# Issuing input loads from the sync engine's queue instead of the scalar engine's

## The chip, the cores and the metric

The kernel runs on one core of a Trainium2 chip. A core has five engines that run their own instruction streams in order and meet only at semaphores: TensorE (PE; its weight loads are shown apart as PEld), VectorE (DVE), ScalarE (ACT), GpSimd (POOL) and SyncE (SP). SP computes nothing here: it issues DMAs. ACT computes and can issue DMAs as well. An instruction that issues a DMA stands in its engine's stream like any other: if it has to wait, everything behind it in that stream waits. The metric is the device time of one execution in microseconds (us).

## The reference

The input `x` has 32 images of 32 channels, 128 x 128, in float32. There are two layers, each of the form x + f(groupnorm(x)), with groups of two channels (16 groups):

```python
x = x + _L0_conv_ref(_gn(x))
x = x + _L1_conv_ref(_gn(x), L1_conv_weights1, L1_conv_weights2)

# layer 0: per 128x128 matrix A, five Newton-Schulz steps towards its square root
Y = A / normA ; Z = I
for _ in range(5):
    T = 0.5 * (3.0 * I - Z @ Y)
    Y = Y @ T
    Z = T @ Z
return Y * sqrt(normA)

# layer 1: 2D FFT, keep 32 x 32 low modes at the top and bottom rows,
# mix the channels with a weight per mode, inverse FFT, real part
top = einsum('bixy,ioxy->boxy', x_dht[:, :, :32, :32], weights1)
bot = einsum('bixy,ioxy->boxy', x_dht[:, :, -32:, :32], weights2)
```

## The kernel before

**Sets.** Layer 0 works on sets of four channels of one image: 32 x 8 = 256 sets, in order. `fetch(b, g)` (line 367) loads a set twice from HBM: as it is (tile `b`, from `in_x`) and transposed (tile `xt`, from `in_xt`), 256 KB each. `staged` (line 375) normalises both in place or into tile `x`: ACT works on `b` and, for images 1 to 18, on half of `x`; POOL does the rest of `x`. `newton` (line 446) is a generator that takes the set through the products on PE, whose results DVE, ACT and POOL take out of PSUM; its last step adds the result to `xt`, and `settle` (line 483) stores `xt` to the scratch tensor `mid` (SP), folds it for layer 1 (POOL) and takes layer 1's statistics (DVE).

**Far and near.** Sets of images 1 to 18 ("far", by `is_far`, line 358) use `far_quartic` (line 421), the others `near_quartic` (line 407). Where the near one transposes on PE, the far one transposes 32 x 32 blocks on DVE (tile `turn`) and moves the blocks between partitions with four DMAs of 64 KB, issued by SP (tile `w <- turn`). A far set does this twice: 144 sets x 8 = 1152 DMAs. After them the set's generator rests four rounds before PE uses `w`.

**Statistics of layer 0.** `prep` (line 223) takes the statistics of one image (the first two) or of a pair of images. It reads the image from HBM in loads of 256 KB, 8 per image (`load`, line 234, tiles `xs`, in four buffers; for the first image four more loads go to `turn` buffers). Three loads are started at the outset and then one more after each load has been read by two `bn_stats` on DVE (`a_st <- xs`). The generator is stepped once a round in the first half of the kernel, every other round later.

**The order of the work** is the program's own: everything is issued through a wrapper (line 89, therefore the line that the profile shows for nearly all instructions) that keeps each engine's instructions in the order in which Python makes them. The main loop (line 1077) runs rounds. In each round it gives one step to each of eight lanes (one lane holds one set), and between the lanes one step to the staging of the next set, to `prep`, and to the queues of layer 1. A lane that takes a new set calls `stage` (line 1016), which begins the normalising of the next set and calls `fetch` for the one after it; so a set is fetched two sets before it starts. A far set starts every 23/8 rounds, a near one every 5.

**Layer 1** runs beside it: `forward` and `spectrum` per image, products with the weights per group of images (20, 7, 3 and 2), then `inverse` per image, which reads `mid` back (`yt`), adds the inverse transform (DVE and POOL) and stores `out`. Its DMAs (`mid`, `yt`, `out`, `ob`, `od`, the weights) are issued by SP; only in the tail ACT issues some.

**Which queue issues what.** Before the change ACT issues `b`, `xt` and `xs` (and `turn` for the first image); SP issues everything else.

Of the kernel before, what the change touches and what calls it, by code (L numbers as in the profile page):

```python
# [94 lines left out]
def conv_preact_kernel(  # L95
# [9 lines left out]
    nc = InOrder(tc)  # L105
# [74 lines left out]
    def bank():  # L180
        return ps8.tile([P, 4, P], F32, tag="ps", name="ps")

    def warm(n):
        ps = bank()
        for _ in range(n):
            nc.tensor.matmul(ps, ident, tab[:, 0:512], start=True, stop=True)

    def root(v, n, s):

        s0 = small.tile([P, n], F32, tag="root_0", name="root_0")  # L190
        nc.scalar.activation(s0, v, AF.Sqrt)
        yield
        q = small.tile([P, n], F32, tag="root_1", name="root_1")
        nc.vector.reciprocal(q, s0)
        nc.vector.tensor_mul(q, q, v)
        nc.vector.tensor_tensor(q, q, s0, ALU.add)
        nc.vector.tensor_scalar_mul(s, q, 0.5)

    def moments(st, ms, tag):

        n = st.shape[1]
        f = st.rearrange("p g (e t) -> p g e t", t=3)
        nc.vector.tensor_reduce(ms, f[:, :, :, 1], AX.X, ALU.add)
        yield from pause
        pm = bank()[:, 0, 0:n]
        nc.tensor.matmul(pm, avg_mean, ms, start=True, stop=True)
        nm = small.tile([P, n], F32, tag=f"{tag}_nm", name=f"{tag}_nm", bufs=2)
        nc.vector.tensor_scalar_mul(nm, pm, 2.0)
        d = small.tile([P, n, 2], F32, tag=f"{tag}_d", name=f"{tag}_d")
        nc.vector.tensor_tensor(  # L210
            d, f[:, :, :, 1], nm[:, :, None].to_broadcast([P, n, 2]), ALU.add
        )
        nc.vector.tensor_mul(d, d, d)
        nc.vector.scalar_tensor_tensor(d, d, 128.0, f[:, :, :, 2], ALU.mult, ALU.add)
        return nm, d
# [4 lines left out]
    def kept(issued):  # L220
        return issued

    def prep(bs, made):

        n = len(bs)
        nc_, ng = n * C, n * G
        first_b = bs[0]
        st = small.tile([P, ng, 6], F32, tag="a_st", name=f"a_st{first_b}", bufs=2)
        tiles = []
        parts = [(b, i) for b in bs for i in range(C // 4)]  # L230

        ahead = 3 if first_b else 8

        def load(k):
            b, i = parts[k]
            if first_b or i < 4:
                t = stp.tile([P, 2, 2 * P], F32, tag="xs", name=f"xs{b}_{i}")
            else:
                t = four("turn", True).rearrange("p (j c) x -> p j (c x)", j=2)
            src = xs_in[b, :, 2 * i : 2 * i + 2].rearrange("p g h c -> p g (h c)")  # L240
            kept(nc.scalar.dma_start(out=t, in_=src))
            tiles.append(t)

        for k in range(ahead):
            load(k)
        yield
        for k in range(len(parts)):
            for j in range(2):
                nc.vector.bn_stats(st[:, 2 * k + j, :], tiles[k][:, j, :])
            yield  # L250
            if k + ahead < len(parts):
                load(k + ahead)
        ms = small.tile([P, ng], F32, tag="a_ms", name=f"a_ms{first_b}")
        nm, d = yield from moments(st, ms, "a")
        yield from pause
        pq = bank()[:, 0, 0:nc_]
        nc.tensor.matmul(pq, avg_mean, d.rearrange("p g c -> p (g c)"), start=True, stop=True)
        if not first_b:
            warm(5)

        v = small.tile([P, nc_ + ng], F32, tag="a_v", name=f"a_v{first_b}")
        nc.vector.tensor_scalar_mul(v[:, 0:nc_], pq, -512 / (P * P))
        yield
        vg = small.tile([P, ng], F32, tag="a_vg", name=f"a_vg{first_b}")
        nc.vector.tensor_reduce(
            vg, v[:, 0:nc_].rearrange("p (g c) -> p g c", c=2), AX.X, ALU.add
        )
        nc.vector.tensor_scalar(v[:, nc_:], vg, 0.5, EPS, ALU.mult, ALU.add)
        yield
        s = small.tile([P, nc_ + ng], F32, tag="a_r_s", name=f"a_r_s{first_b}", bufs=2)  # L270
        yield from root(v, nc_ + ng, s)
        iv = small.tile([P, nc_ + ng], F32, tag="a_inv", name=f"a_inv{first_b}")
        nc.vector.reciprocal(iv, s)
        yield

        sc = small.tile([P, nc_], F32, tag="a_sc", name=f"a_sc{first_b}", bufs=2)
        nc.vector.tensor_scalar_mul(sc, iv[:, 0:nc_], MS / P)
        off = small.tile([P, ng, 2], F32, tag="a_off", name=f"a_off{first_b}", bufs=2)
        nc.vector.tensor_tensor(
            off,  # L280
            sc.rearrange("p (g c) -> p g c", c=2),
            nm[:, :, None].to_broadcast([P, ng, 2]),
            ALU.mult,
        )
        off = off.rearrange("p g c -> p (g c)")
        sn = small.tile([P, nc_], F32, tag="a_t_s", name=f"a_t_s{first_b}", bufs=3)
        for k, b in enumerate(bs):
            g, c = slice(k * G, k * G + G), slice(k * C, k * C + C)
            made[b] = (nm[:, g], sc[:, c], off[:, c], sn[:, c])
        yield  # L290
        nn = small.tile([P, ng, 2], F32, tag="a_d", name=f"a_n{first_b}")
        nc.vector.tensor_tensor(
            nn,
            s[:, 0:nc_].rearrange("p (g c) -> p g c", c=2),
            iv[:, nc_:, None].to_broadcast([P, ng, 2]),
            ALU.mult,
        )
        nn = nn.rearrange("p g c -> p (g c)")
        for far in sorted({is_far(b) for b in bs}):
            of = [k for k, b in enumerate(bs) if is_far(b) == far]  # L300
            c = slice(of[0] * C, of[-1] * C + C)
            f = EYE_Q * QS if far else EYE * QF
            nc.vector.tensor_scalar_mul(nn[:, c], nn[:, c], P * (1.5 / f) ** 2)
        yield
        yield from root(nn, nc_, sn)
        yield
# [6 lines left out]
    def four(tag, more):  # L313
        n, m = rooms[tag]
        shape = [P, 4, 2, P] if tag == "my" else [P, 4, P]
        if more:
            turns[tag] += 1
            if turns[tag] % (n + m) >= n:
                return early.tile(shape, F32, tag=tag + "_early", name=tag, bufs=m)
        return sets.tile(shape, F32, tag=tag, name=tag, bufs=n)  # L320
# [37 lines left out]
    def is_far(b):  # L358
        return 0 < b < FIRST

    def has_more(b, g):

        return b * (C // 4) + g < MORE
# [2 lines left out]

    def fetch(b, g):
        xt, t = four("xt", has_more(b, g)), four("b", has_more(b, g))
        kept(nc.scalar.dma_start(out=t, in_=x[b, :, 4 * g : 4 * g + 4, :]))
        kept(nc.scalar.dma_start(out=xt, in_=xt_in[b, :, 4 * g : 4 * g + 4, :]))  # L370
        raw[b, g] = xt, t

    norms = []
# [642 lines left out]
    def stage():  # L1016

        b, g = stages.pop(0)
        if g == 0:
            while b not in made:  # L1020
                step(preps)
        while coming and (b, g) >= coming[0][0]:
            preps.append(prep(coming.pop(0)[1], made))
        norms.append(staged(b, g, *made[b]))
        if fetches:
            fetch(*fetches.pop(0))
# [45 lines left out]
    step(preps)  # L1072
    coming = [((0, 0), [1])] + [((b - 2, 4 if b < FIRST else 2), [b, b + 1]) for b in range(2, B, 2)]
    fetch(*fetches.pop(0))
    stage()
    fetch(*fetches.pop(0))
    while todo or any(lanes) or posts or specs or prods or backs:
        tail = not todo and not any(lanes)
        if early and len(settled) >= MORE:
            change()  # L1080
        for i in range(LANES):
# [5 lines left out]
            if lanes[i] is None and todo and room and rounds >= due:  # L1087
# [3 lines left out]
                b, g = todo.pop(0)  # L1091
                xt = ready[0][0]
# [5 lines left out]
            if lanes[i] is not None:  # L1098
                b, g, xt, steps = lanes[i]
# [86 lines left out]
```

## Time and profile before

Three runs took 3022.42 us in the median (3022.03 to 3023.22). The profiled execution took 3016.65 us.

| what | value |
|---|---|
| profiled execution, its span | 3016.65 us, 3014.7 us |
| PE, PEld busy | 2897.6 us, 2689.0 us |
| DVE, POOL, ACT busy | 2321.8 us, 1995.8 us, 1652.1 us |
| queue of SP: packets, MB, share of the 16 DMA engines | 328512, 347.77, 38.7% |
| queue of ACT: the same | 113616, 208.45, 22.2% |
| `w<-turn` issues on SP | 1152 of 64 KB |
| `b<-in_x`, `xt<-in_xt` issues on ACT | 256 and 256 of 256 KB |
| `xs<-in_xs` issues on ACT | 252 of 256 KB |

How to read it: an engine's busy time does not count the issuing of DMAs or the waiting for semaphores. In the lists of waits a line names the engine and the tile that it was about to work on, then what ended its idle time, the total in us, how often, and the longest. `SPq` and `ACTq` are the issuing sequencers of SP and ACT. In the lines in order of time the columns are start (us from the span's start), duration (us), engine, operation, tiles, count, and in square brackets the idle time before and what ended it. All instructions are shown at line 89, the wrapper; so tiles tell them apart.

### The profile page before, as it was taken

To read this page: it belongs to the slowest core of one execution; us is meant where nothing else is said; L and a number is where in the kernel's file an instruction comes from. 1 tells how busy PE (TensorE), PEld (TensorE's weight loads), DVE (VectorE), ACT (ScalarE), POOL (GpSimd) and SP (SyncE) were. 2 spreads that over 40 slices of the span, in tenths; PEclk is the share of its full clock that TensorE was granted. 3 is DMA by queue.
4 is the path that set the end of the run, shared out by engine and by line. 5 is a ranking of instruction groups with operands and counts; after the bars stand their busy time and mean duration, and the time that the engine had idled before them with its cause. 6 is when DMAs were issued, how large, how long until landed. Compare 5 with 4: busy or idle time off the path is not lost.

```text
span 3014.7 us, 73315 instructions
## 1 busy us (share of the span) xinstructions
PE 2897.6 (96%) x27112; PEld 2689.0 (89%) x27112; DVE 2321.8 (77%) x4262; ACT 1652.1 (55%) x4187; POOL 1995.8 (66%) x2308
## 2 busy tenths in 40 slices
PE   7999999999999999999999999999989999999995
PEld 7899999999999999999999889888878899888884
DVE  7778898989888888889876645777886767776564
ACT  4566666566565656566554445455544544665452
POOL 4676777777777767777765434787777763678352
PEclk9999999999999999999999999999999999999997
DMA  5465655556565656565633566777877737676576
GB/s 176 135 176 145 171 163 153 167 152 180 134 192 135 192 131 195 142 183 140 190 102 99 158 209 208 257 247 254 271 235 245 252 121 225 203 242 216 175 230 242
DMA packets 442482, 560.91 MB, mean 186 GB/s; under 512 B 99344, under 2 KB 260112, under 8 KB 442128
## 3 DMA queue, kind: packets, MB, share of 16 engines
q1 hardware_dynamic: 328512, 347.77, 38.7%
q10 hardware_dynamic: 113616, 208.45, 22.2%
q8 instruction: 218, 3.57, 0.5%
q14 instruction: 136, 1.11, 0.1%
HBM read 326.93 MB, written 153.62 MB: 159 GB/s over the span
## 4 chain that ended last, share of the span: by engine, by line
PE 71%; POOL 8%; DVE 7%; DMA 7%; issue 5%; SPq 1%; ACT 1%; ACTq 0%; POOLq 0%; DVEq 0%
PE ps L89 71%; POOL yt L89 3%; POOL r L89 2%; POOL x L89 1%; POOL fold L89 1%; DMA yt<-mid 1%; SPq L89 1%; DVE turn L89 1%; DVE root L89 1%; DMA w<-turn 1%; DMA out<-yt 1%; DVE v L89 1%; DVE yt L89 1%; DVE a_d L89 1%; DMA xs<-in_xs 1%
## 5 line engine op out<-in xcount | busy, mean ns | idle before, releaser
L89 PE MATMUL ps<-my,q 128*128 128x128 f32 (+1 forms) x4096 | 747.0, 330 | 16.6 <-DVE q L89 9.9
L89 PEld LDWEIGHTS ps<-my,q 128*128 128x128 f32 x4096 | 623.0, 192 | 67.7 <-issue 7.4
L89 PE MATMUL ps<-w,v 128*128 128x128 f32 x4096 | 555.4, 279 | 19.6 <-DVE w L89 15.3
L89 ACT ACTIVATE b<-b,a_off,a_sc 128x128 f32<-128x128 f32 x1024 | 469.7, 491 | 166.2 <-issue 57.0
L89 ACT ACTIVATE my<-ps 128x512 f32<-128x512 f32 x512 | 306.2, 599 | 428.3 <-PE ps L89 408.9
L89 POOL TENSOR_TENSOR fold<-xt 128x256 f32<-128x256 f32 x512 | 363.4, 731 | 261.5 <-DVE xt L89 248.9
L89 PEld LDWEIGHTS ps<-w,v 128*128 128x128 f32 x4096 | 502.9, 193 | 32.5 <-DVE w L89 13.9
L89 POOL TENSOR_TENSOR yt<-yt,d 128x512 f32<-128x512 f32 x244 | 306.5, 1279 | 223.2 <-ACT d L89 195.5
L89 ACT ACTIVATE t<-ps 128x256 f32<-128x256 f32 x512 | 192.0, 381 | 311.7 <-PE ps L89 298.4
L89 DVE STREAM_TRANSPOSE turn<-v 128x512 f32<-128x512 f32 x288 | 326.1, 1132 | 9.9
L89 POOL TENSOR_SCALAR x<-xt,a_nm,a_sc 128x128 f32<-128x128 f32 x736 | 321.4, 450 | 15.6 <-DVE a_sc L89 15.4
L89 POOL TENSOR_TENSOR mb<-eye_q,mb 128x512 f32<-128x512 f32 x144 | 184.0, 1278 | 197.8 <-ACT y L89 139.2
L89 ACT ACTIVATE y<-ps,a_t_s 128x128 f32<-128x128 f32 x1024 | 290.4, 374 | 0.0
L89 POOL TENSOR_TENSOR v<-eye_v,x 128x512 f32<-128x512 f32 x144 | 184.0, 1278 | 143.8 <-ACT x L89 136.7
L89 PE MATMUL ps<-q,t 128*128 128x128 f32 x2048 | 273.9, 277 | 4.3 <-ACT t L89 3.7
L89 PE MATMUL ps<-x,b 128*128 128x128 f32 x2048 | 277.7, 279 | 0.0
L89 PE MATMUL ps<-x,q 128*128 128x128 f32 x2048 | 274.7, 277 | 3.0 <-DVE w L89 2.0
L89 DVE SCALAR_TENSOR_TENSOR v<-ps,v 128x512 f32<-128x512 f32 x288 | 195.1, 678 | 104.5 <-PE ps L89 101.8
L89 PE MATMUL ps<-y,t 128*128 128x128 f32 x2048 | 274.5, 277 | 0.1
L89 PE MATMUL ps<-my,mb 128*128 128x128 f32 x2048 | 272.2, 276 | 0.0
L89 PEld LDWEIGHTS ps<-my,mb 128*128 128x128 f32 x2048 | 257.9, 192 | 9.6 <-issue 1.6
L89 PEld LDWEIGHTS ps<-x,q 128*128 128x128 f32 x2048 | 249.4, 192 | 14.1 <-issue 8.4
(131 smaller groups left out, 5074.9 us busy)
## 6 DMA issues: line engine op xcount, KB each, us to landing
w<-turn SPq DMA_DIRECT2D x1152, 64.0 KB
b<-in_x ACTq DMA_DIRECT2D x256, 256.0 KB
xt<-in_xt ACTq DMA_DIRECT2D x256, 256.0 KB
mid<-xt SPq DMA_DIRECT2D x256, 256.0 KB
yt<-mid SPq DMA_DIRECT2D x128, 512.0 KB
xs<-in_xs ACTq DMA_DIRECT2D x252, 256.0 KB
out<-yt SPq DMA_DIRECT2D x115, 512.0 KB
plain<-in_wk SPq DMA_DIRECT2D x34, 512.0 KB
```

The lines of the kernel that those rows point to most:

```text
L89: return self.tc.keep_in_program_order(issue(*args, **kw))
```

## The change

Three calls that issue loads name the sync engine where they named the scalar engine. They stand at the same places of the source.

```diff
@@ prep, load(k)
             src = xs_in[b, :, 2 * i : 2 * i + 2].rearrange("p g h c -> p g (h c)")
-            kept(nc.scalar.dma_start(out=t, in_=src))
+            kept(nc.sync.dma_start(out=t, in_=src))
             tiles.append(t)
@@ fetch(b, g)
         xt, t = four("xt", has_more(b, g)), four("b", has_more(b, g))
-        kept(nc.scalar.dma_start(out=t, in_=x[b, :, 4 * g : 4 * g + 4, :]))
-        kept(nc.scalar.dma_start(out=xt, in_=xt_in[b, :, 4 * g : 4 * g + 4, :]))
+        kept(nc.sync.dma_start(out=t, in_=x[b, :, 4 * g : 4 * g + 4, :]))
+        kept(nc.sync.dma_start(out=xt, in_=xt_in[b, :, 4 * g : 4 * g + 4, :]))
         raw[b, g] = xt, t
```

## The prediction

> **What bounds the kernel now.** I read the busy totals first, then the stages, then who waits for whom, then two places in order of time.
>
> The page's first part and its chain:
>
> ```profile
> span 3014.7 us, 73315 instructions
> PE 2897.6 (96%) x27112; PEld 2689.0 (89%) x27112; DVE 2321.8 (77%) x4262; ACT 1652.1 (55%) x4187; POOL 1995.8 (66%) x2308
> PE 71%; POOL 8%; DVE 7%; DMA 7%; issue 5%; SPq 1%; ACT 1%; ACTq 0%; POOLq 0%; DVEq 0%
> ```
>
> TensorE is busy 96%; the scalar engine and its queue hold 1% and 0% of the chain, so freeing them cannot bring much. Busy time by stage (PE, PEld, DVE, ACT, POOL, then clock, DMA share, GB/s):
>
> ```profile
> 450.00:610.00 160.00, 159.27 (x1333) 151.22 (x1332) 139.02 (x245) 97.42 (x250) 116.23 (x129) 1.00 0.59 162
> 2080.00:2350.00 270.00, 256.51 (x2270) 231.27 (x2268) 210.54 (x386) 139.29 (x366) 205.37 (x234) 0.98 0.78 258
> ```
>
> There are two regimes. From 130 to 1510 us (images 1 to 18, one pair of images every 160 us) PE idles 0.7 us of 160, DVE is 87% busy, ACT 61%. After 1510 us PE idles some 5%. Over the whole span, gaps of more than 0.3 us in which neither PE nor its weight loads run sum to 89 us: 9 us between 130 and 1510, 53 between 1510 and 2790, 21 after, 6 before 130. A gain can only come out of these; a loss can come anywhere.
>
> Waits between 290 and 1410 us, DVE's and SP's own:
>
> ```profile
> DVE a_st L89 <- DMA xs<-in_xs: 10.0, 12, 1.7
> SPq L89 <- DVE turn L89: 354.0, 105, 7.1
> ```
>
> DVE already meets the statistics' loads (xs) late 12 times. SP spends 354 us waiting for a block's `turn` tile: a load put behind such a wait inherits it. One such place, in order of time:
>
> ```profile
> 349.73 0.33 ACTq L89 DMA_DIRECT2D xs<-in_xs  x1
> 349.97 6.28 SPq L89 DMA_DIRECT2D w<-turn  x8
> ...
> 353.46 0.75 DVE L89 BATCH_NORM_STATS2 a_st<-xs 128x6 f32<-128x256 f32 x2 [0.88 <-DMA xs<-in_xs]
> ```
>
> And one where the present order hurts:
>
> ```profile
> 2300.58 1.02 ACTq L89 DMA_DIRECT2D xs<-in_xs  x2
> 2301.65 0.60 ACT L89 ACTIVATE my<-ps 128x512 f32<-128x512 f32 x1 [7.78 <-issue]
> ...
> 2302.30 1.99 PEld L89 LDWEIGHTS ps<-my,q 128*128 128x128 f32 x9 [4.51 <-ACT my L89]
> ```
>
> ACT stood 7.8 us before a copy out of PSUM because two loads ahead of it in its stream could not issue, and PE then idled 4.1 us.
>
> **What the Trainium skill says.** "DMA: Bandwidth & Descriptors", section "Anatomy of one DMA": the engines that move data do not wait on semaphores; the wait is on the issuing sequencer before dispatch. The trace agrees: the 7.8 us above. Same page, "Issuing engines are not separate DMA queues": transfers of all issuers interleave on the same 16 engines, so only the sequencer's time is saved. No bandwidth is to be won, then; both queues together use 61% of the engines' time here (38.7 + 22.2). Same page, "Queues, rings and completion order": SP and ACT own one ring each, served in turn packet by packet. After the change the loads and the `w` transfers share one ring, in order.
>
> **The change, part by part.** The listings of the two builds show PE, DVE and POOL instructions in the same order; 768 DMAs (256 `b`, 256 `xt`, 252 `xs`, 4 `turn`) leave ACT's stream and stand in SP's at the same places of the program. Nothing is added or dropped. Both builds have eight completion counters for all DMAs, so each issue may also wait for an earlier landing.
>
> *ACT's side, removed.* 126 + 92 + 91 us of issue (xt 256 x 493 ns, b 256 x 359, xs 252 x 361). Between 130 and 1510 us this lies beside PE work and is worth nothing: PE has 9 us of gaps there, none over 0.8 us after 132 us. After 1510 us the gaps that follow a held ACT are 4.1 us (2298), 2.5 (1901, ACT held 6.1 us for an `out` landing) and 0.7 (2081): 7.3 us. Bounds 0 to 12; I take -7. In the start-up ACT holds the second image's xs loads behind work (22.2, 24.5, 27.4, 29.3 us); SP has nothing before them but first loads. PE's gaps there are 6 us, of which I take -2.5 (bounds 0 and -4; the table's load now stands ahead of the first xs, at 0.4 us).
>
> *SP's side, added.* Some 0.35 to 0.42 us for each moved load: 1.1 us per 10 us block, beside 8 x 0.6 + 0.5 = 5.4 us of present issues. SP has room (about 56% to 67% used), so the point is order. I laid ACT's and SP's recorded issues into the after build's order, each no earlier than the one before it ended.
>
> - `b` and `xt`: issue 3 us later at the median, at most 6.5, and some earlier. From landing (each transfer's last packet) to first use they have at least 10.6 us, mostly 17. Hidden by two blocks of other work.
> - `w`: last issue 0.8 us later at the 90th percentile, 1.7 at most. From landing to its matmul it has 1.7 us at least, 3.3 at 5%, 6.1 at the median. Alone, hidden. Behind it stand PE's matmuls ps<-w,v.
> - `mid` stores: 0.4 us later at the 75th percentile, 2.3 at most; nothing in the near work waits.
> - `xs`: this is the one. At 349.7 us the three first loads of a pair move behind a group of four `w`, whose own wait ends at 349.97: by the recorded durations to 353.4, 353.8, 354.2, so 3.6, 3.3 and 3.1 us later. The first landed 1.1 us before its use at 353.46; now DVE, in order, stands about 2.5 us. Over 130 to 1510 us the 144 xs loads go 2.3 us later at the median, 4.6 at 90%; 51 of them overrun their slack, by 91 us together and 4.2 at most. After 1510 us none overruns (SP reaches them earlier than ACT did).
>
> *Where the DVE stall goes.* Queued behind the waiting statistics are the q, t, v and turn of all lanes. PE starts on a q 1.4 to 1.5 us after DVE ends it in the tightest tenth, about 3 us at the median. DVE's own gaps (132 us over 1120) give some of the lateness back: 0.7 us every 6. Carrying each overrun through these gaps and slacks gives PE 11 us lost in nine pairs; 5 if every xs lands 1 us earlier, 23 if 1 us later. The ring order (a `w` now stands behind up to three 256 KB loads, each about 0.7 to 0.9 us of packets) is not in this and adds to it; I take +15, bounds 0 and 30. In the late stages the shared ring puts xs behind 512 KB `yt` and `out` transfers: +2 (0 to 6).
>
> Sum: -7 - 2.5 + 15 + 2 = +7.5 us on the profiled execution's 3016.65 (span 3014.7 and 1.95 around it). The median of the runs, 3022.42, is 5.8 above that execution; the same difference on it gives 3030.
>
> **Rivals.** *Faster.* The rests between a lane's steps swallow DVE's lateness (far-stage loss 3 or less) and what is left is ACT's release: -2.5 - 7, a little more in the last third, 3011. For it: median slacks of 3 and 6 us against a median xs lateness of 2.3. Against it: the overruns come at the head of each pair, where the gap in PE's stream already is. It decides if xs issues under about 1 us later. *No change.* Both sides near 8 us, or neither: 3022. *Much slower.* SP falls behind, so that `w` lands more than 3 us later at each block rather than 0.8; each such us is a PE us, some 3 us per pair and more: 3060. Against it: SP is two thirds used. *Nothing done* is excluded: the listing shows the 768 instructions moved.
>
> **How the numbers follow.** A measurement of this kernel tells about 0.2%, 6 us, from no change. Slower as summed 0.40 (own range 3028 to 3042), much slower 0.08, no change 0.26, faster 0.26. So slower 0.48, same 0.26, faster 0.26. The range 3008 to 3046 leaves out the much slower case and the outer ends of the bounds.
>
> **What would show it.** Right: ACT's stream without ACTq loads; DVE's waits for xs up from 10 us to 60 or more between 290 and 1410; the pairs' period up from 160 us by 1 to 2; no 7.8 us hold of ACT near 2300 and fewer PE gaps from 1870 to 2350. Wrong: an unchanged 160 us period with DVE waits up (the rests hide it: faster), or PE waiting for `w` transfers in most blocks (SP behind: much slower). New waits of SP for counters, with `b` later than 17 us, would be a cause that I have not priced.

## The result and the profile after

Four runs of the changed kernel took 3063.88 us in the median (3063.14 to 3065.13), four of the kernel before on the same chip 3022.23 us. The ratio is 1.0141 (95% interval 1.0124 to 1.0159): slower, as forecast, but by 42 us where I had said 7.5, and outside my range. The profiled execution took 3065.13 us, 48.5 more than the one before, which had lain 5.6 us under its median; so the two profiles differ by 7 us more than the medians do.

From the page of the changed kernel, span, busy time, chain and the queue that now carries nearly all transfers:

```profile
span 3063.3 us, 73569 instructions
...
PE 2911.2 (95%) x27112; PEld 2691.3 (88%) x27112; DVE 2328.9 (76%) x4262; ACT 1639.9 (54%) x4187; POOL 2000.0 (65%) x2308
...
q1 hardware_dynamic: 439104, 549.15, 59.9%
...
PE 65%; DVE 12%; DMA 8%; issue 5%; POOL 5%; SPq 4%; ACT 0%; DVEq 0%; ACTq 0%; POOLq 0%
```

The busy totals hardly moved: no engine got more work. In the chain SP's queue went from 1% to 4% and DVE from 7% to 12%, while PE fell from 71% to 65%; in the chain by line, `DMA xs<-in_xs` went from 1% to 4%. So a wait grew, and it lies at SP and DVE.

Where it lies is seen by following one event through both traces: the end of DVE's instruction that adds a set's result to `xt`. I call a set a block here and number the 256 of them from 0. After minus before, in us: -2.8 at block 7, +64.6 at block 151, +48.9 at block 255. Some 67 us were lost in the far part (images 1 to 18) and 16 won back after it. In the far part a pair of images took 160.2 us before and 167.8 after (means of seven pairs, blocks 23 to 135).

Busy time by stage in the changed kernel, the same two stretches and columns as before:

```profile
450.00:610.00 160.00, 153.21 (x1257) 144.34 (x1256) 130.46 (x233) 91.99 (x239) 112.67 (x125) 1.00 0.59 156
2080.00:2350.00 270.00, 259.99 (x2327) 234.79 (x2320) 210.70 (x373) 143.04 (x376) 208.34 (x239) 0.99 0.77 253
```

In the first stretch PE now idles 6.8 us of 160 (0.7 before) at the same clock and DMA share; in the second it idles less (10.0 of 270, 13.5 before; the same clock time now holds work that came some 50 us sooner before).

Two waits of the kernel before between 290 and 1410 us:

```profile
DVE v L89 <- PE ps L89: 80.2, 75, 2.5
...
PE ps L89 <- DVE q L89: 2.0, 6, 0.3
```

Waits of the changed kernel in the same stretch:

```profile
DVE a_st L89 <- DMA xs<-in_xs: 92.5, 37, 4.0
...
DVE v L89 <- PE ps L89: 57.6, 55, 2.5
...
PE ps L89 <- DVE q L89: 19.4, 23, 2.0
...
PE ps L89 <- DVE v L89: 12.5, 11, 1.9
...
PE ps L89 <- DMA w<-turn: 1.1, 2, 0.6
```

DVE's wait for the statistics' loads went from 10.0 to 92.5 us. Its waits for PE, which could have made room, fell less: the largest of them, on `v`, from 80.2 to 57.6. PE now waits for DVE's `q` and `v`, 32 us together (2.0 and nothing before), and almost never for `w`.

One pair's statistics in order of time (the place that answers to 349.7 to 353.5 us before):

```profile
353.96 3.02 SPq L89 DMA_DIRECT2D w<-turn  x4
...
357.02 1.56 SPq L89 DMA_DIRECT2D xs<-in_xs  x3
...
360.14 0.75 DVE L89 BATCH_NORM_STATS2 a_st<-xs 128x6 f32<-128x256 f32 x2 [3.56 <-DMA xs<-in_xs]
...
373.85 1.08 SPq L89 DMA_DIRECT2D xs<-in_xs  x2
...
377.49 0.75 DVE L89 BATCH_NORM_STATS2 a_st<-xs 128x6 f32<-128x256 f32 x2 [2.12 <-DMA xs<-in_xs]
...
380.55 0.67 DVE L89 SCALAR_TENSOR_TENSOR q<-ps,mb 128x512 f32<-128x512 f32 x1
...
381.37 1.96 PE L89 MATMUL ps<-my,q 128*128 128x256 f32 x8 [1.18 <-DVE q L89]
```

The three first loads stand behind four `w` issues, as forecast, and DVE stands 3.56 us at the head of the pair. PE shows no gap there: the first one over 1 us in this pair comes 20 us later, behind the second stall. Each pair has such a stall at its head and four or five of 1.1 to 3.2 us within the next 51 us; they sum to 12.5 to 14.0 us per pair (1.4 before, and 10.1 more forecast).

### The profile page after: what moved, and what is told of

It is laid out like the page before. It is cut to its first block, busy times and chain, and to the rows that moved or that the text cites. A ratio compares the mean times of both kernels' runs of the same rounds, so it can differ in the third digit from the quotient of the medians.

```text
span 3063.3 us, 73569 instructions
## 1 busy us (share of the span) xinstructions
PE 2911.2 (95%) x27112; PEld 2691.3 (88%) x27112; DVE 2328.9 (76%) x4262; ACT 1639.9 (54%) x4187; POOL 2000.0 (65%) x2308
## 4 chain that ended last, share of the span: by engine, by line
PE 65%; DVE 12%; DMA 8%; issue 5%; POOL 5%; SPq 4%; ACT 0%; DVEq 0%; ACTq 0%; POOLq 0%
PE ps L89 65%; SPq L89 4%; DMA xs<-in_xs 4%; DVE v L89 2%; POOL yt L89 2%; DVE turn L89 1%; POOL r L89 1%; DVE yt L89 1%; DVE a_st L89 1%; DVE root L89 1%; DMA w<-turn 1%; DVE q L89 1%; POOL fold L89 1%; POOL x L89 1%; DVE a_d L89 1%
## 5 line engine op out<-in xcount | busy, mean ns | idle before, releaser
L89 DVE BATCH_NORM_STATS2 a_st<-xs 128x6 f32<-128x256 f32 x504 | 186.1, 413 | 127.7 <-DMA xs<-in_xs 127.5
L89 ACT COPY mb<-ps 128x512 f32<-128x512 f32 x256 | 150.5, 588 | 209.7 <-PE ps L89 194.4
```

Source lines behind the costliest of these rows:

```text
L89: return self.tc.keep_in_program_order(issue(*args, **kw))
```

## The experiments

All runs are compared with the kernel before on the same chip; it took 3014.32, 3016.63 and 3012.23 us in the three groups of runs, and the groups were run on different chips. "Far" is what the profiled execution had lost or won at block 151, "end" at block 255, both against the one profile of the kernel before, which is from another chip than those of the runs. Each rests on one execution, and runs of one kernel lie up to 15 us apart (3006.28 to 3021.54 for the kernel before in the first group), so a few us there say little alone. The wait is DVE's for `xs` over seven pairs, blocks 23 to 135.

| kernel | ratio (95%) | pair, us | wait, us (times) | far | end |
|---|---|---|---|---|---|
| before | 1 | 160.2 | 10.0 (12) | 0 | 0 |
| after | 1.0141 (1.0124-1.0159) | 167.8 | 94.1 (38) | +64.6 | +48.9 |
| 1 statistics only | 1.0210 (1.0185-1.0234) | 168.8 | 102.4 (35) | +80.4 | +66.1 |
| 2 sets only | 0.9974 (0.9964-0.9985) | 160.3 | 18.2 (17) | +5.7 | -10.7 |
| 3 after, earlier xs, idle step | 1.0023 (1.0015-1.0030) | 159.9 | 4.3 (9) | -10.2 | -1.8 |
| 4 the same on ACT | 1.0073 (1.0054-1.0091) | 159.6 | 0 | -9.7 | +17.8 |
| 5 after, earlier xs | 0.9949 (0.9934-0.9964) | 160.5 | 37.6 (19) | +2.9 | -12.5 |
| 6 as 3, idle step in the first part only | 0.9918 (0.9895-0.9942) | 160.1 | 3.1 (8) | -7.8 | -23.1 |
| 7 as 6, xs on ACT | 0.9952 (0.9937-0.9967) | 159.9 | 0 | -1.4 | -9.6 |
| 8 before, one load less ahead | 1.0053 (1.0036-1.0071) | 161.1 | 42.9 (39) | +5.6 | +8.4 |
| 9 before, 7 banks | 1.0070 (1.0053-1.0086) | 161.0 | 10.6 (12) | +4.6 | +12.0 |
| 10 after, idle step only | 1.0060 (1.0044-1.0075) | 163.7 | 49.7 (30) | +32.6 | +16.2 |
| 11 as 8, 7 banks | 1.0129 (1.0112-1.0146) | 162.0 | 45.7 (42) | +12.2 | +34.9 |

My theory after the result, theory A: the statistics' loads are late because SP reaches them behind `w` issues that wait for DVE; DVE stands, PE follows, and the sets' loads have no part in it. Its rivals: the sets' loads fill SP's stream and delay everything, or the shared ring makes the transfers themselves slow. A later question was why so little of DVE's lateness was swallowed.

### Which of the moved loads costs (runs 1 and 2)

Run 1 moves the statistics' loads alone:

```diff
-            kept(nc.scalar.dma_start(out=t, in_=src))
+            kept(nc.sync.dma_start(out=t, in_=src))
```

> Only the statistics' loads (xs) go to SP; b and xt stay on ACT. Theory A (the late xs alone costs): between blocks 8 and 151 it loses what the full change lost there, 65 us or nearly (55 to 70), the period of a pair is about 168 us, and DVE waits some 90 us for xs between 290 and 1410 us; after that it gains perhaps 5 to 10 us of the 16; time about 3070 (3060 to 3080). Theory B (crowding: all 768 loads delay SP's w issues, whichever they are): the loss is shared by number, 252 of 768, some 20 us; time about 3040.

Run 2 moves the two loads of the sets alone:

```diff
-        kept(nc.scalar.dma_start(out=t, in_=x[b, :, 4 * g : 4 * g + 4, :]))
-        kept(nc.scalar.dma_start(out=xt, in_=xt_in[b, :, 4 * g : 4 * g + 4, :]))
+        kept(nc.sync.dma_start(out=t, in_=x[b, :, 4 * g : 4 * g + 4, :]))
+        kept(nc.sync.dma_start(out=xt, in_=xt_in[b, :, 4 * g : 4 * g + 4, :]))
```

> Only b and xt go to SP; xs stays on ACT. Theory A: no loss between blocks 8 and 151 (0 to 5 us), DVE's waits for xs there at 10 to 15 us as before, and a part of the late gain (5 to 10 us) stays; time 3010 to 3020, not slower than before. Theory B: two thirds of the 65 us remain, time about 3050.

Measured: 1.0210 and 0.9974. DVE's wait in the list of waits of run 1, between 290 and 1410 us:

```profile
DVE a_st L89 <- DMA xs<-in_xs: 95.7, 33, 4.3
```

The same of run 2:

```profile
DVE a_st L89 <- DMA xs<-in_xs: 18.2, 17, 3.1
```

The statistics' loads alone bring the whole loss, and more of it than the full change. A good part of the surplus goes with PE's granted clock, the share of its full clock that the profile shows PE to be given: between blocks 7 and 151 run 1 took 12.6 us longer than the changed kernel; its clock was at half for 37.5 us there against 6.8, which is worth up to 15 us (see the last section), and PE's gaps were 7 us longer. Why it has more of both is not shown. The sets' loads, 512 of the 768, cost the far part 5.7 us at the most (4.2 of them before block 8) and win 16.4 after it. Late gains do not add: run 1 wins 14.3 from block 151 to the end, run 2 16.4, both together 15.7.

### Taking the lateness away (runs 3 and 4)

Run 3 is the changed kernel with the next load issued ahead of the step's end rather than at the start of the next step, and with one idle step after a pair's first three loads, so that every load has about one round more.

```diff
         yield
+        if first_b:
+            yield
         for k in range(len(parts)):
             ...
-            yield
             if k + ahead < len(parts):
                 load(k + ahead)
+            yield
```

> The full change, but each xs load is issued one round earlier (right after the statistics of an earlier tile instead of one step later, and one idle step of the generator after the first three loads), with the same four buffers. Theory A (lead time of xs against SP's order): one round is some 3.5 us more lead, which covers most overruns: DVE's waits for xs fall below 20 us between 290 and 1410, the pair period returns to 160 to 162 us, time 3005 to 3020. Theory C (the shared ring or the queue's load makes transfers slow): no more than 10 us is won back, about 3055.

Run 4 makes the same edit to the kernel before, so on ACT's queue.

> Control: the kernel before with the same earlier xs loads, on ACT. Theory A: the kernel before loses almost nothing to xs (10 us of DVE waits, covered), so within 0.3% of it: 3015 to 3028. If it gains as much as the third run gains on the full change, the earlier loads are worth something by themselves and the third run proves less.

Measured: 1.0023 and 1.0073. In run 3 DVE's wait between 290 and 1410 us falls to

```profile
DVE a_st L89 <- DMA xs<-in_xs: 4.3, 9, 0.9
```

The pair's period falls to 159.9 us, and the far part is 10 us faster than before rather than 65 slower, with all 768 loads on SP. That is what theory A says, and neither rival can be the cause: SP's stream is as full and the ring as shared as in the changed kernel. The control, run 4, shows that the earlier loads do little by themselves: on ACT they win 9.7 us in the far part, where run 3 wins 75 against the changed kernel. The landing times agree: from issue to last packet an `xs` load takes 3.3 us before, 3.2 in the changed kernel and 3.1 in run 3, in the median.

The end was a miss for run 4 (3036.52 us, where 3015 to 3028 was expected), and takes back run 3's gain: both lose two steps of some 9 us late (run 3 between blocks 191 and 199 and between 223 and 231), run 4 some more. The first of them in order of time, run 3:

```profile
2163.12 2.49 POOL L89 TENSOR_TENSOR yt<-yt,d 128x512 f32<-128x512 f32 x2
...
2163.91 6.66 DVE L89 TENSOR_TENSOR a_d<-a_st,a_nm 128x64 f32<-128x64 f32 x1
...
2169.23 1.25 POOL L89 TENSOR_TENSOR r<-mb,eye 128x512 f32<-128x512 f32 x1
...
2171.02 0.69 DVE L89 SCALAR_TENSOR_TENSOR q<-ps,eye 128x512 f32<-128x512 f32 x1
...
2171.76 2.08 PE L89 MATMUL ps<-y,t 128*128 128x128 f32 x8 [6.26 <-DVE q L89]
```

One small DVE instruction of the statistics takes 6.66 us, behind it `q` is late, and PE idles 6.26 us. The other 3 us of the step are the granted clock. Two stretches of run 3 (us, busy PE, PEld, DVE, ACT, POOL, then clock, DMA share, GB/s):

```profile
2158.00:2168.00 10.00, 7.50 (x68) 6.52 (x66) 7.87 (x8) 4.23 (x11) 10.00 (x12) 1.00 0.36 128
2168.00:2175.00 7.00, 3.24 (x12) 3.03 (x13) 6.90 (x10) 0.00 (x0) 2.71 (x4) 0.52 0.49 148
```

For 6.8 us from 2168 the clock is at half, and the eight matmuls at 2171.76 take 2.08 us, where eight of this shape take 1.06 elsewhere. The idle step shifts the statistics by one step, which late in the kernel is two rounds, and so onto a run of POOL instructions (see the last section). It has nothing to do with the queues.

### The two halves of the edit (runs 5, 6 and 7)

Run 5 is run 3 without the idle step.

> The full change; the later xs loads of an image or pair one round earlier, the first three unchanged (no idle step after them). Theory A: only the first overrun of each pair stays (DVE stands some 3 to 4 us at its head, once per pair), so DVE's waits for xs between blocks 23 and 135 are 20 to 35 us instead of 94 and the pair period is 161 to 163 us. In the late part it should not show the two steps of 9 us of the third run, if the idle step (which makes a pair's statistics end later) caused them. Time 3005 to 3030. Theory C (ring or queue load): 3050 or more.

Run 6 is run 3 with `if first_b and early:` ahead of the idle step, which limits it to the first part of the kernel, where the statistics step in every round.

> As the third run, but the idle step only in the first part (while the early pool is open). Theory A: no xs waits in the far part (period 160) and, if the idle step caused the late loss of the third run, none of that either: 2995 to 3010. If the late steps of 9 us stay, they come from the earlier loads or from the order that they make, not from the idle step: about 3015 to 3021.

Run 7 is run 6 with the statistics' loads back on ACT.

> b and xt on SP, xs on ACT and one round earlier, idle step only in the first part. Against the second run (0.9974 of before): if what the full change gains late comes from taking xs off ACT as well, this one stays near the second run, 3000 to 3010; if early xs on ACT hold ACT less (they wait for statistics of a round before), 2995 to 3003. It tells whether the version with everything on SP or the divided one is better.

Measured: 0.9949, 0.9918 and 0.9952. The 9 us steps are in none of the three; the idle step late in the kernel was their cause. Run 5's waits came a little above the 20 to 35 us expected, its period below the 161 to 163, and run 6's time 2 us under its range. Run 6 beats both kernels: 2993.01 us in the median (2986.96 to 2999.80) against 3016.63. Its stretch in the far part, and two of its waits between 290 and 1410 us:

```profile
450.00:610.00 160.00, 158.86 (x1331) 150.62 (x1330) 139.15 (x246) 96.40 (x250) 116.89 (x128) 1.00 0.59 162
```

```profile
PE ps L89 <- DVE q L89: 3.8, 7, 0.6
DVE a_st L89 <- DMA xs<-in_xs: 3.1, 8, 0.8
```

It has PE's far part of the kernel before and the late part of the changed one (-15.3 us from block 151 to the end). Run 7 has -8.2 there: with the early loads, issuing `xs` on SP rather than ACT is worth some 7 us late. Its trace has a reason: the hold near 2300 us is back. An `xs` issue in ACT's stream ended only at 2297.15 us; by then ACT had stood 6.2 us before the `my` behind it, and PE stood 3.9. Run 6 has no such gap. No run of 7 was as fast as the slowest of 6 (2999.95 and 2999.80 us). So in the profiled executions both moved kinds help the late part; only the place of the `xs` issues in SP's order was harmful.

Run 5 carries the first hint on how lateness passes to PE. It still has one stall of 3.0 to 4.3 us at each pair's head (nothing precedes the first loads of a pair there) and little else, 37.6 us in seven pairs, and its period is 160.5 us, only 0.3 more than before. Three of its waits between 290 and 1410 us:

```profile
DVE a_st L89 <- DMA xs<-in_xs: 37.6, 19, 4.3
...
PE ps L89 <- DVE a_d L89: 2.9, 7, 0.4
PE ps L89 <- DVE q L89: 2.8, 8, 0.5
```

A stall of 3 to 4 us with only one of some 1.5 us behind it cost PE next to nothing here. Whether that is because it is nearly alone or because of its place at the head of the pair, no run tells apart.

### Late loads without SP (run 8)

The kernel before with two loads ahead rather than three, all on ACT; each load is issued one round later.

```diff
-        ahead = 3 if first_b else 8
+        ahead = 2 if first_b else 8
```

> The kernel before, nothing on SP, but only two xs loads ahead instead of three, so that each load is issued one round (3.5 us) later against its use. Theory A (late xs alone is the cause, SP's order only makes them late): DVE's waits for xs between blocks 23 and 135 rise from 10 us to 70 to 140, the pair period to 166 us or more, and the far part loses 40 to 100 us; time 3050 to 3110. If the loss needs SP (its order or its w transfers), the far part loses less than 10 us.

Measured: 1.0053, a miss. DVE's wait between 290 and 1410 us:

```profile
DVE a_st L89 <- DMA xs<-in_xs: 42.9, 39, 3.2
```

A round less of lead on ACT makes the loads less late than SP's order does: 39 waits, but of 1.1 us each, 42.9 us together, where 70 to 140 were expected. The period rises by 0.9 us per pair for 4.7 us more of waits. So lateness of the loads alone, without SP, does lengthen the period, and these small stalls cost a fifth of their sum. But the far part lost only 6.7 us from block 7 on, under the 10 that were to mean that the loss needs SP. As the stalls were half as large as in the changed kernel, the run does not decide whether lateness of the same size on ACT would cost as much.

### Does the head stall make the later ones? (run 10)

In the changed kernel SP issues `w` 0.06 us after DVE has ended `turn` (median), so SP moves with DVE. The four later stalls could then follow from the first (theory "inherited"), or have their own cause and add up (theory E). Run 10 is the changed kernel with the idle step alone, in the first part, so that the head stall goes and the order of the later loads stays.

```diff
         yield
+        if first_b and early:
+            yield
```

> The full change with only the idle step after the first three xs loads of a pair (first part); the later loads at their old places. It takes away the stall at the head of each pair (3.5 us) and nothing else. Theory E (each overrun has its own cause, w groups ahead of it in SP's order, and they add up): the later stalls stay, DVE's waits for xs between blocks 23 and 135 are 60 to 80 us, pair period 163 to 167, time 3020 to 3050. Theory F (feedback: the head's stall makes DVE late, DVE makes SP's w late, and that makes the later xs late): the later stalls go too, waits below 40 us, period 160 to 161.5, time about 3000.

Measured: 1.0060, period 163.7 us, both as theory E had it; the waits, 49.7 us, lie between the two theories' ranges. The head stall is gone in seven pairs of eight, and four later ones stay at 14 to 46 us after the head, in sum 7.1 us per pair (9.9 for the four in the changed kernel). Its waits between 290 and 1410 us:

```profile
DVE a_st L89 <- DMA xs<-in_xs: 49.7, 30, 3.2
...
PE ps L89 <- DVE v L89: 11.1, 10, 2.2
...
PE ps L89 <- DVE q L89: 6.3, 13, 0.5
```

So the later stalls have their own cause, and they cost by themselves: 5.7 us of stall more than before, 3.5 us of period. They shrink by a quarter, so a part may have been inherited. With the head stall in front of them (the changed kernel) 12.0 us more cost 7.7; nearly the same head stall without them (run 5) costs 0.3. The cost is not in proportion to the sum of the stalls, which I had not seen.

### Is it the ring of PSUM banks? (runs 9 and 11)

PE's gaps behind `v` stand at products `my,q` and `q,t`, which do not read `v`; what they can wait for is the bank that `v` was read from (the banks are the parts of PSUM, the memory that PE writes its products to). If that ring (`bank`, eight buffers) passes the lateness on, theory D, one bank less should make late loads dearer. Run 9 is the kernel before with seven, run 11 is run 8 with seven.

```diff
-    ps8 = ctx.enter_context(tc.tile_pool(name="ps8", bufs=8, space=PSUM))
+    ps8 = ctx.enter_context(tc.tile_pool(name="ps8", bufs=7, space=PSUM))
```

> The kernel before with seven PSUM banks in its ring instead of eight. Theory D (the ring of banks is one of the two ways in which DVE's lateness reaches PE): with one bank less PE is nearer to waiting for a bank, so the far part's pair period rises from 160.2 by 1 to 6 us, with PE gaps ended by DVE or ACT reading a bank. If banks are plentiful, the period stays at 160.2 and the way over the banks is doubtful.

> Seven banks and only two xs loads ahead, on ACT. With eight banks the late loads cost 0.9 us per pair. Theory D: with seven, the same stalls of DVE cost clearly more against the seven-bank kernel without them: 3 us per pair or more. If the banks are not the way, about 1 us again.

Measured: 1.0070 and 1.0129. Seven banks alone lengthen the pair by 0.8 us (160.2 to 161.0), just short of the 1 to 6 that theory D gave. With eight banks the late loads cost 0.9 us per pair (run 8), with seven 1.0 (162.0 against 161.0). The ring is not what decides there, so theory D is not supported. But run 8's stalls are small, and the test says little on the long ones of the changed kernel; how much of its loss passes through the banks stays open.

## Why the prediction was right and wrong, step by step

**ACT's and SP's sides, and the order: right.** The loads stand where the reading of the two orders put them. The first load of the pair at 349.7 us was forecast 3.6 us late at its issue; against DVE's own shift of 4.0 us it was 3.3 us late. DVE was to start about 2.5 us later there, on top of the 0.88 that it had stood before; it stood 3.56. `b` and `xt` are hidden (run 2). `w` is nearly so: PE waited 1.1 us in all for it. The time from a `turn` to its first `w` issue went from 0.95 to 2.06 us at the 90th percentile; its slack from landing to use, at the least, from 1.0 (one group; the next has 1.5, and the prediction had read 1.7) to 0.5 us. The "much slower" rival came near the number, 3060, for a reason that is not there, so by luck: SP does not fall behind with `w`.

**The sizes.** The start was put at -2.5 us and came to -2.8. DVE's stalls were put at 91 us more for nine pairs, 10.1 each, and grew by 12.0 each, from 1.4 to 13.4: a fifth more. The slack that the overruns were held against was too large: it ran from a load's last packet to its use, and where DVE already stood waiting in the kernel before, it started only 0.7 us after the last packet (median of 16 waits of over 0.5 us), so that this much of it was no slack. At 349.7 us the 1.1 us were counted although DVE had stood idle for that very load. The ring was said to add to the stalls; in the far part the landing times of `xs` fell from 3.3 to 3.0 us in the median, so this clause was wrong, and the fall hid a part of the error in the slack. (`b` took 0.5 us longer and stayed hidden.)

**Where the DVE stall goes: the step that failed.** It is the term of +15 us. I carried each overrun through DVE's gaps and slacks and found 11 us lost to PE in nine pairs; I took +15, with 30 as the upper bound. It was +67 from block 7 to block 151. In the balance of one pair, 12.0 us more of stalls, DVE's waits for PE give back 4.2 (they fall from 118.8 to 89.5 us in seven pairs, with `q`, `t` and `xt` beside `v`), and the period takes 7.7. Before, DVE's waits for PE were 17 us per pair. My working treated them all as room in which a lateness goes out again. Only a quarter was: for the rest I take it that PE's own lateness brings the data later as well, so that the wait is still there. Nor may a later overrun be counted only as far as it exceeds the lateness that is there: SP issues `w` and then `xs` behind DVE's `turn`, so the next load shifts with the stall. Run 10 shows that the later stalls have causes of their own. With stalls of 10.1 us more per pair and the passing rate measured (7.7 of 12.0), the same forecast would have been +58 in nine pairs.

The profile before showed the warning. PE idled 0.7 us of 160, DVE was busy 87%, and its waits for PE came in some 160 pieces of 0.4 to 1.1 us in the mean (seven pairs). A DVE that waits for a saturated PE, whose next work hangs on DVE again, is no idle DVE.

**What the far part's loss looks like at PE.** Gaps of over 0.3 us between blocks 7 and 151 sum to 6.7 us before and 51.1 after. That is 44 of the 67 us. The granted clock was at half for 6.8 us there, which is 3.4 more; the other 20 lie within the time that the profile counts as busy, and since the ends of matmuls are modelled I cannot say where.

**The late part: ACT's release right, the rest missed.** I took -7 for ACT's release and +2 for the shared ring; from block 151 to the end it was -15.7. Of PE's gaps of over 0.3 us there (58.5 before, 47.0 after) those that ended with ACT's `my` went from 9.5 to 1.6 us: the 7 us forecast. The hold of 7.8 us near 2300 and the ones of 6.1 and 4.1 at 1901 and 2091 us are not in the changed kernel. Other gaps bring 3.6 more. Of the 4.2 that are not gaps, 3.4 are the granted clock, which was at half for 30.7 us rather than 37.5. The +2 did not come: DVE waited no longer for `xs` there (3.3 us before, 0.6 after). So the sum -7 - 2.5 + 15 + 2 came to -15.7 - 2.8 + 67.4 and nothing for the last.

**The rivals.** "Faster" was to need `xs` issues under about 1 us late; the 3.3 us at the pair shown are not that, and the rests did not swallow the lateness. "Against it: the overruns come at the head of each pair" was upside down: run 5 shows the head stall to be nearly free where little follows it, and run 10 the ones behind it to be dear. The test "period up by 1 to 2 us" showed the error at once: it was up by 7.7.

## What to carry to other kernels

A DMA moved to another engine's queue inherits every wait that stands ahead of it there, so list those waits before counting issue time; here 252 loads behind `w` issues that wait for DVE cost 2%, while 512 loads with two blocks of lead gained 0.3%. Do not count an engine's waits for the saturated engine as room for its own delays: where the two feed each other, a good part of the stalls may be paid. Here stalls of 1 to 4 us, five or six in a pair, were paid to 64% of what they added, four of 1 to 3 us to 61%, ones of 1.1 us to a fifth, and a nearly lone one of 3 to 4 us hardly. And mend the lead, not the queue: with one round more for the late loads the same change wins 0.8%.

## What the runs showed of the hardware

**A small DVE instruction can stand through a run of POOL instructions.** Single small DVE instructions of the statistics take some 6 us, where they take 0.2 us undisturbed, when they start inside a run of POOL `TENSOR_TENSOR` instructions that follow each other without a gap. The kernel before, in order of time:

```profile
2201.47 2.51 POOL L89 TENSOR_TENSOR yt<-yt,d 128x512 f32<-128x512 f32 x2 [5.54 <-ACT d L89]
...
2201.61 1.21 DVE L89 TENSOR_SCALAR a_r_s<-root 128x96 f32<-128x96 f32 x1
...
2208.24 2.52 POOL L89 TENSOR_TENSOR yt<-yt,d 128x512 f32<-128x512 f32 x2
...
2209.61 6.08 DVE L89 TENSOR_SCALAR a_sc<-a_inv 128x64 f32<-128x64 f32 x1
...
2210.70 1.28 POOL L89 TENSOR_TENSOR r<-b,eye 128x512 f32<-128x512 f32 x1
...
2211.93 2.50 POOL L89 TENSOR_TENSOR yt<-yt,d 128x512 f32<-128x512 f32 x2
...
2214.36 1.28 POOL L89 TENSOR_TENSOR r<-mb,eye 128x512 f32<-128x512 f32 x1
...
2216.70 1.62 PE L89 MATMUL ps<-my,q 128*128 128x256 f32 x3 [5.07 <-DVE q L89]
```

The DVE instruction of 6.08 us ends at 2215.69, POOL's run at 2215.64, and PE has idled 5.07 us. In run 3 the one of 6.66 us ends at 2170.57 and POOL's run at 2170.48. The Trainium skill, "SBUF — State Buffer", section "Who interferes with whom", says that DVE and GpSimd share a pair of ports as an exclusive lock; a DVE instruction with two SBUF inputs contends for it with a GpSimd instruction that reads SBUF, one in a mode that uses both ports contends with GpSimd too, and whoever issues first has it for the whole instruction while the other is blocked. The blocking agrees with these rows; whether the `TENSOR_SCALAR` ran in such a mode the profile does not say. Its length goes further than one instruction: the DVE instruction stood through what was left of five, 1.28 us each at most.

In the thirteen traces 57 small DVE instructions took over 2 us, and each ended within 0.12 us of the end of a POOL `TENSOR_TENSOR` behind which POOL paused or went on with another operation. Starting in such a run is not enough, however: the one at 2201.61 above took 1.21 us although POOL's next followed without a gap, and of some 380 small ones (0.3 us or less at their fastest) that started during a POOL `TENSOR_TENSOR` in the kernel before, about 290 took less than 1 us and two over 2 us. What decides stays open. There are two over 2 us in the kernel before and four in the changed one, but nine each in runs 3 and 4, and three and four in runs 5 and 6: they appeared and went with one idle step of a generator.

**A PE gap costs more than itself.** The granted clock of PE goes to half for 3.4 or 6.8 us at a time. In the thirteen traces there are 118 such stretches between blocks 7 and 255, and every one began during a PE gap of over 1 us or within 3.5 us of its end. Counted so, a stretch at half clock came with 5 of the 151 gaps of 1 to 1.5 us, 48 of the 72 of 2 to 3 us, and all 23 of 4.5 us or more. So the gap of 6.26 us in run 3 came with a step of 9. That the gap brings the clock down is read from this order of events; no run varied it alone.
